# Non-local blocks in fp32: softmax denominators of two query pairs in one product, pooled products at every second pair

## The chip, the cores and the metric

The kernel runs on one core of a Trainium2 chip. The metric is the device time of one execution in microseconds (us), lower is better. Times come from repeated executions; one further execution was recorded by the hardware profiler. All data and all products are fp32.

The engines that matter here: PE multiplies matrices and writes PSUM, ACT (ScalarE) does exponentials, copies and biases, DVE (VectorE) does sums, maxima, reciprocals, and SP only issues DMAs. Each runs its own instructions strictly in the order in which the program lists them, and waits for the others by semaphores.

## The reference

Two layers are applied, one after the other, to x of shape (4, 128, 96, 96). A layer is (both layers alike, each with its own weights):

```python
g_x     = maxpool2(conv1x1(x, g_w, g_b)).reshape(b, CI, -1).transpose(0, 2, 1)    # 2304 keys x 64
theta_x = conv1x1(x, theta_w, theta_b).reshape(b, CI, -1).transpose(0, 2, 1)      # 9216 queries x 64
phi_x   = maxpool2(conv1x1(x, phi_w, phi_b)).reshape(b, CI, -1)                   # 64 x 2304 keys
f    = jnp.einsum('bqc,bck->bqk', theta_x, phi_x)
attn = jax.nn.softmax(f, axis=-1)
y    = jnp.einsum('bqk,bkc->bqc', attn, g_x)
W_y  = conv1x1(y, W_w, W_b)          # then a batch norm with fixed mean and variance
return W_y * inv + shift + x
```

So for each of 4 images and 2 layers: queries from all 9216 positions, keys and values from a 2 x 2 max-pooling of 9216 positions to 2304, attention over all keys, a projection, and the input added.

## The kernel before, in words

**Blocks, pairs, batches.** An image in a layer is a block; there are eight, in the order `ORDER`, so that an image's second layer never follows directly on its first. A block's 9216 queries are nine *pairs* (`NP`) of two times 512 queries, 72 pairs in all. A pair goes over the 2304 keys in 18 tiles of 128 (`NKT`), two at a time (`KB`): nine *batches* (`NB`), numbered j = 0 to 8.

**A batch.** `scores(k)` (L288 on PE) multiplies phi and theta into a PSUM tile `sc` of 128 x 1024, keys by queries, in four 64 x 64 tiles of the array side by side. ACT takes exp of it (L294), DVE adds the exp tile to a running `sum` (L298, L300). One batch later `values(k)` (L308) multiplies the exp tile by the pooled values into the accumulator `av`, again in four 64 x 64 tiles. There are two `sc` buffers, nine exp buffers, one `av`. PE's order in the main loop is: scores of batch t, then values of batch t-1, then what else is due.

**After a pair.** The softmax denominator is the sum over keys of `sum`: `denominators` (L321) multiplies it by a 128 x 64 matrix of ones, two products of 128 rows by 64 columns of the array side by side, one for each half of the queries; each result stands in 64 rows, so that it can multiply the output elementwise. ACT copies `av` to `halves` (L315), and copies the denominators to `rc` and adds them up for a later range check (L332). DVE adds the two halves (L345), takes the reciprocal of `rc` (L336, four pieces) and multiplies (L347); all that is in `normalise`. `note` (L341, ACT) adds up the reciprocals for the check. `project` (L356, PE) multiplies by W in 64 x 64 tiles, DVE adds shift and input (L362) in place into x, and in the second layer SP stores the piece (L367).

**The visit.** Everything that needs all 128 rows of the array at once comes together, once per pair, after the values of its batch 0 (`J_WINDOW`): up to three products of the next block's keys and values (`pooled`: L197 on PE into a `misc` PSUM tile, max-pooled by DVE at L203; there are two such tiles), the denominators of the pair before, and theta of the pair after (L275), which ACT copies out with its bias (L282). Denominators and theta share one `sc` buffer if there are such products in the visit, and take the two `misc` tiles otherwise. When enough of the next block is pooled, `spread` (three times per block, six transposes at L242, a DVE copy at L245, ACT at L232 and L235) brings it into its final layout, in the same place. The projection of the pair before follows in batch 4 (`J_PROJECT`).

```python
            if j == J_WINDOW:
                others = list(steps.pop(q % NP, []))
                for step in others[:2]:
                    step()
                visit(q, len(others) > 1)
                for step in others[2:]:
                    step()
                if q:
                    pairs[q - 1].normalise()
```

There are 24 products per block (`CC` = 384 columns each), three per visit (`CHUNKS`), so eight of a block's nine visits have some; the second block's come by fours in six visits. The last block's visits have none. The first block is prepared ahead of and within the first batches. SP's only work after the start is 39 stores and the loads of x, six pieces each (L94).

Of the kernel before, what the change touches and what calls it, by code (L numbers as in the profile page):

```python
# [9 lines left out]
F32 = mybir.dt.float32  # L10
I32 = mybir.dt.int32
AF = mybir.ActivationFunctionType
# [4 lines left out]
P = 128  # L17
# [16 lines left out]
NP = HW // PT  # L34
KB = 2
NB = NKT // KB
J_WINDOW, J_PROJECT = 0, 4
CHUNKS = 3
FIRST_CHUNKS, FIRST_GT = 4, 3
WARM = 5  # L40
ORDER = ((0, 0), (1, 0), (0, 1), (2, 0), (1, 1), (3, 0), (2, 1), (3, 1))
SHIFT = 35.0
SUM_MIN, SUM_MAX = 1e-20, 1e30
# [3 lines left out]
def shifted_blocks(ctx: ExitStack, tc: tile.TileContext, x: bass.AP, layers, out: bass.AP, flag):  # L47
# [38 lines left out]
    nc.vector.memset(ones, 1.0)  # L86
    dens = const.tile([P, len(ORDER) * NP], F32, name="dens")
    recs = const.tile([P, len(ORDER) * NP], F32, name="recs")

    def load_x(b, n=6):  # L90
        xt = xp.tile([C, HW], F32, tag="x", name=f"x_{b}")
        src = x[b].rearrange("c h w -> c (h w)")
        for i in range(n):
            nc.sync.dma_start(out=xt[:, ts(i, HW // n)], in_=src[:, ts(i, HW // n)])  # L94
        return xt
# [13 lines left out]
    class Layer:  # L109


        def __init__(self, l, p):
            self.l, self.p, self.col = l, p, {}
# [67 lines left out]
    class Block:  # L181
# [69 lines left out]
            self.spread_phi(i)  # L251
            self.spread_g(i)

        def key_steps(self, first, chunks):

            steps = {}
            for r in range(HW // CC):
                steps.setdefault(first + r // chunks, []).append(lambda r=r: self.pooled(r))
            for i in range(NKT // GT):
                last = ((i + 1) * GT * KT * 4 // CC - 1) // chunks  # L260
                steps.setdefault(first + last + 1, []).append(lambda i=i: self.spread(i))
            return steps

    class Pair:

# [12 lines left out]
                )  # L278

        def take_theta(self, ps):  # L280
            self.th = work.tile([P, QT], F32, tag="theta", name=f"theta_{self.name}")
            nc.scalar.activation(self.th, ps, AF.Identity, bias=self.blk.w.col["theta_b"])  # L282

        def scores(self, k):
            ps = ps_sc.tile([P, PT], F32, tag="sc", name=f"sc_{self.name}_{k}")
            for c in range(2):
                for h in range(2):
                    nc.tensor.matmul(  # L288
                        ps[ts(c, CI), ts(h, QT)],
                        lhsT=self.blk.phi[ts(h, CI), ts(2 * k + c, CI)],  # L290
                        rhs=self.th[ts(h, CI), :], start=True, stop=True,
                    )
            e = work.tile([P, PT], F32, tag="exp", name=f"exp_{self.name}_{k}", bufs=9)
            nc.scalar.activation(e, ps, AF.Exp, bias=nshift)  # L294
            self.es[k] = e
            if k == 1:
                self.sum = work.tile([P, PT], F32, tag="sum", name=f"sum_{self.name}")
                nc.vector.tensor_add(self.sum, self.es[0], e)  # L298
            elif k > 1 and not (self.last and k == NKT - 1):
                nc.vector.tensor_add(self.sum, self.sum, e)  # L300

        def values(self, k):
            if k == 0:
                self.av = ps_av.tile([P, PT], F32, tag="av", name=f"av_{self.name}")
            e = self.es[k]
            for h in range(2):
                for r in range(2):
                    nc.tensor.matmul(  # L308
                        self.av[ts(h, CI), ts(r, QT)], lhsT=self.blk.gT[ts(r, CI), k, :],
                        rhs=e[ts(r, CI), ts(h, QT)],  # L310
                        start=(k == 0), stop=(k == NKT - 1),
                    )
            if k == NKT - 1 and not self.last:
                self.halves = work.tile([P, PT], F32, tag="halves", name=f"halves_{self.name}", bufs=1)
                nc.scalar.copy(self.halves, self.av)  # L315

        def denominators(self, ps):
# [5 lines left out]
                        start=(i == 0), stop=(i == len(parts) - 1),  # L323
                    )

        def take_denominators(self, ps):
            self.den, n = ps, self.number
            self.rc = work.tile([P, QT], F32, tag="rc", name=f"rc_{self.name}", bufs=1)
            if self.last:
                self.inverses(ps)  # L330
            else:
                nc.scalar.activation(self.rc, ps, AF.Identity, accum_out=dens[:, n : n + 1])  # L332

        def inverses(self, src):
            for i in range(QT // P):
                nc.vector.reciprocal(self.rc[:, ts(i, P)], src[:, ts(i, P)])  # L336

        def note(self):
            n = self.number
            to = self.th if self.last else self.rc  # L340
            nc.scalar.activation(to, self.rc, AF.Identity, accum_out=recs[:, n : n + 1])  # L341

        def normalise(self):
            self.y = y = self.halves[:, :QT]
            nc.vector.tensor_add(y, y, self.halves[:, QT:])  # L345
            self.inverses(self.rc)
            nc.vector.tensor_mul(y, y, self.rc)  # L347

        def project(self):

# [15 lines left out]
                cols = ts(self.p, PT)  # L366
                nc.sync.dma_start(out=self.blk.store[:, cols], in_=self.blk.xt[:, cols])  # L367

        def finish(self, check, result):

            n = QT // 2
            halves = work.tile([P, PT], F32, tag="halves", name=f"halves_{self.name}", bufs=1)
            y, half = halves[:, :QT], halves[:, QT:]
            nc.scalar.copy(half, self.av[:, QT:])
            nc.vector.tensor_add(y, self.av[:, :QT], half)
            for i in range(2):
                nc.vector.tensor_mul(y[:, ts(i, n)], y[:, ts(i, n)], self.rc[:, ts(i, n)])
            nc.scalar.activation(
                self.th, self.den, AF.Identity, accum_out=dens[:, self.number : self.number + 1]
            )  # L380
            self.note()
            pss = [
                ps_sc.tile([P, PT], F32, tag="sc", name=f"W_ps_{self.name}_{i}") for i in range(2)
            ]
# [9 lines left out]
            for i in range(2):  # L394
# [8 lines left out]
                if i == 0:  # L403
                    result()

    ws = [Layer(l, p) for l, p in enumerate(layers)]
    ws[0].load_gphi((nc.scalar, nc.sync))
    xs = {0: load_x(0, 12)}
# [16 lines left out]
        store = out[b].rearrange("c h w -> c (h w)") if l else None  # L425
        blocks.append(Block(None, ws[l], store, f"{b}_{l}"))

    def begin(n, gt):

        b, l = ORDER[n]  # L430
        if b not in xs:
            xs[b] = load_x(b)
        blocks[n].xt = xs[b]
        blocks[n].begin_keys(gt)

    pairs = [Pair(blk, p, n * NP + p) for n, blk in enumerate(blocks) for p in range(NP)]
    total = len(pairs) * NB

    def visit(n, shared=True):

        if shared:
            ps = ps_sc.tile([P, PT], F32, tag="sc", name=f"den_theta_ps_{n}")
            den, th = ps[:, :QT], ps[:, QT:]
        else:
            den = ps_misc.tile([P, QT], F32, tag="misc", name=f"den_ps_{n}")
            th = ps_misc.tile([P, QT], F32, tag="misc", name=f"theta_ps_{n}")
        if n > 0:
            pairs[n - 1].denominators(den)
        if n + 1 < len(pairs):
            pairs[n + 1].theta(th)  # L450
        if n > 0:
            pairs[n - 1].take_denominators(den)
        if n + 1 < len(pairs):
            pairs[n + 1].take_theta(th)


    warm = ps_misc.tile([P, QT], F32, tag="misc", name="warm_ps")
    for i in range(WARM):
        nc.tensor.matmul(warm[:, :P], lhsT=ident, rhs=ident, start=True, stop=True)


    begin(0, FIRST_GT)
    b0 = blocks[0]
    ws[0].make_gphi()
    ws[0].make_theta()
    b0.pooled(0)
    b0.pooled(1)
    b0.pooled_2(2)
    first_cols()
    for w in ws:  # L470
        w.make_std()
    nc.scalar.preload_act_table(AF.Exp)
    b0.spread_phi(0)
    visit(-1)
    b0.pooled(4)
    b0.pooled(5)
    b0.pooled_2(6)
    b0.spread_phi(1)
    b0.spread_g(0)
    between = {0: 8, 1: 12, 3: 16, 4: 20}  # L480
    after = {
        0: [lambda: b0.spread_g(1)],
# [6 lines left out]
        NB: [ws[1].make_gphi, ws[1].make_theta],  # L489
        2 * NB: [ws[1].make_W, ws[1].make_shift],  # L490
    }
    steps = {}
    for t in range(total + 1):
        if t < total:
            q, j = divmod(t, NB)
            if q % NP == 0 and j == 0 and q // NP + 1 < len(blocks):
                begin(q // NP + 1, GT)
                plan = (2, FIRST_CHUNKS) if q == 0 else (0, CHUNKS)
                steps = blocks[q // NP + 1].key_steps(*plan)
            for k in range(j * KB, (j + 1) * KB):  # L500
                pairs[q].scores(k)
        if t in between:
            b0.pooled(between[t])
            b0.pooled(between[t] + 1)
            b0.pooled_2(between[t] + 2)
        if t:
            q, j = divmod(t - 1, NB)
            if j == J_PROJECT and q:
                pairs[q - 1].note()
                pairs[q - 1].project()  # L510
            if t <= total:
                for k in range(j * KB, (j + 1) * KB):
                    pairs[q].values(k)
            if t == total - 1:
                visit(len(pairs))
            if t == total:
                break
            if j == J_WINDOW:
                others = list(steps.pop(q % NP, []))
                for step in others[:2]:  # L520
                    step()
                visit(q, len(others) > 1)
                for step in others[2:]:
                    step()
                if q:
                    pairs[q - 1].normalise()
        for step in after.pop(t, []):
            step()

    good = const.tile([P, 2], F32, name="good")  # L530
    count = const.tile([1, 2], F32, name="count")
# [11 lines left out]
        nc.vector.tensor_scalar(count[:, 1:2], count[:, 0:1], 2.0 * P, None, ALU.is_lt)  # L543
        nc.vector.tensor_copy(flag, count[:, 1:2])

    pairs[-1].finish(check, result)


@with_exitstack
# [301 lines left out]
```

## Time and profile before

| | |
|---|---|
| time, median of 3 runs (lowest to highest) | 2609.92 us (2609.47 to 2610.31) |
| the profiled execution's own time | 2608.83 us |
| its span in the profile | 2606.8 us |
| DVE sum, one addition of 128 x 1024 (L300) | 1224 ns, x1151 |
| exp, one tile of 128 x 1024 (L294) | 1113 ns, x1296 |
| reciprocal, 128 x 128 (L336) | 908 ns, x284 |
| max-pooling of one product (L203) | 552 ns, x192 |
| granted clock of TensorE, mean | 0.999 of full speed |

How to read it: a timeline line gives the start and the duration in us, the engine, the line of the kernel, the operation and its operands, how many instructions are merged, and in brackets the idle time before and what ended it. `PE` rows are matmuls, `PEld` rows their weight loads, which run ahead. An fp32 matmul of the program is two matmuls in the profile. The ends of matmuls are modelled, so the distance from one start to the next is the more reliable measure of a matmul's time. Each profile line's "mean ns" is of one instruction; in 64 x 64 tiles four run at once, in 128 x 64 tiles two.

### The profile page before, as it was taken

The page shows a single profiled execution, that of the slowest core. Times are in us where ns is not written, and L with a number is a line of the kernel's source. Part 1 is how long each engine was busy: PE and PEld are TensorE (multiplying, and loading weights), DVE is VectorE, ACT ScalarE, POOL GpSimd, SP SyncE. Part 2 cuts the span into 40 slices and gives each one's busy share as a digit, 9 for nine tenths or more (in the row PEclk, how much of TensorE's full clock was granted, in tenths as well). Part 3 has the DMA queues.
Part 4 walks back from the last instruction along what each step waited for, and adds up shares of the span by engine and source line. Part 5 has one row for each costly group of instructions (what it writes and reads, how often), then busy time and mean ns, then how long its engine had stood idle before and what let it go on. Part 6 is the DMA issues. An engine that isn't in the chain of part 4 may idle for free.

```text
span 2606.8 us, 52190 instructions
## 1 busy us (share of the span) xinstructions
PE 2585.5 (99%) x22836; PEld 908.6 (35%) x22836; DVE 2036.2 (78%) x2069; ACT 1625.5 (62%) x1786; POOL 0.7 (0%) x6
## 2 busy tenths in 40 slices
PE   9999999999999999999999999999999999999998
PEld 3333333333333333333333333333333333333332
DVE  5777787777787777887778877778777788777777
ACT  4666666666666666666666666666666666666665
POOL 0000000000000000000000000000000000000000
PEclk9999999999999999999999999999999999999999
DMA  5000000000000002000000000000000000000000
GB/s 222 1 1 1 1 1 1 1 1 1 1 18 9 18 17 89 2 1 1 1 1 18 17 10 17 17 2 1 1 1 1 18 17 17 9 17 18 17 17 26
DMA packets 10974, 41.41 MB, mean 16 GB/s; under 512 B 1514, under 2 KB 2420, under 8 KB 10740
## 3 DMA queue, kind: packets, MB, share of 16 engines
q1 hardware_dynamic: 10572, 37.96, 3.7%
q8 instruction: 180, 2.95, 0.4%
q14 instruction: 54, 0.44, 0.1%
q10 hardware_dynamic: 168, 0.07, 0.0%
HBM read 19.14 MB, written 18.87 MB: 15 GB/s over the span
## 4 chain that ended last, share of the span: by engine, by line
PE 95%; DVE 2%; ACT 2%; issue 0%; DMA 0%; ACTq 0%; DVEq 0%
PE sc L288 42%; PE av L308 41%; PE gphi_ps L197 5%; PE W_ps L356 2%; PE den_theta_ps L321 2%; PE den_theta_ps L275 2%; ACT exp L294 1%; DVE sum L300 1%; PE theta_ps L275 1%; DVE sum L298 0%; PE den_ps L321 0%; ACT phi L232 0%; DVE centre L230 0%; ACT phi L235 0%; DVE gphi L203 0%
## 5 line engine op out<-in xcount | busy, mean ns | idle before, releaser
L294 ACT ACTIVATE exp<-sc,nshift 128x1024 f32<-128x1024 f32 x1296 | 1375.4, 1113 | 701.3 <-PE sc L288 700.7
L300 DVE TENSOR_TENSOR sum<-sum,exp 128x1024 f32<-128x1024 f32 x1151 | 1409.4, 1224 | 320.6 <-ACT exp L294 240.9
L288 PE MATMUL sc<-theta,phi 64*64 64x512 f32 x10368 | 1234.7, 591 | 5.5 <-ACT exp L294 4.6
L308 PE MATMUL av<-exp,gT 64*64 64x512 f32 x10368 | 1229.1, 589 | 0.0
L308 PEld LDWEIGHTS av<-exp,gT 64*64 64x64 f32 x10368 | 395.9, 133 | 716.5 <-issue 696.0
L288 PEld LDWEIGHTS sc<-theta,phi 64*64 64x64 f32 x10368 | 385.7, 133 | 721.5 <-issue 649.2
L336 DVE RECIPROCAL rc<-rc 128x128 f32<-128x128 f32 x284 | 240.2, 908 | 0.7
L298 DVE TENSOR_TENSOR sum<-exp,exp 128x1024 f32<-128x1024 f32 x72 | 88.2, 1226 | 136.8 <-ACT exp L294 136.8
L203 DVE TENSOR_REDUCE gphi<-gphi_ps 128x96 f32<-128x384 f32 x192 | 100.4, 552 | 95.0 <-PE gphi_ps L197 94.4
L332 ACT ACTIVATE rc<-den_theta_ps 128x512 f32<-128x512 f32 x54 | 32.3, 597 | 191.0 <-PE den_theta_ps L275 191.0
L197 PE MATMUL gphi_ps<-x,gphiT 128*64 128x384 f32 x768 | 148.5, 500 | 0.0
L362 DVE SCALAR_TENSOR_TENSOR x<-W_ps,shift,x 128x512 f32<-128x512 f32 x142 | 99.6, 743 | 0.0
L315 ACT COPY halves<-av 128x1024 f32<-128x1024 f32 x71 | 71.9, 1012 | 32.2 <-PE av L308 32.2
L197 PEld LDWEIGHTS gphi_ps<-x,gphiT 128*64 128x64 f32 x768 | 50.5, 138 | 107.9 <-issue 62.3
L356 PE MATMUL W_ps<-halves,WT 64*64 64x512 f32 x568 | 73.7, 589 | 0.0
L321 PE MATMUL den_theta_ps<-sum,ones 128*64 128x512 f32 x220 | 56.6, 593 | 0.0
L275 PE MATMUL den_theta_ps<-x,thetaT 128*64 128x512 f32 x216 | 55.5, 592 | 0.0
L347 DVE TENSOR_TENSOR halves<-halves,rc 128x512 f32<-128x512 f32 x71 | 49.1, 692 | 2.4
L345 DVE TENSOR_TENSOR halves<-halves 128x512 f32<-128x512 f32 x71 | 48.5, 683 | 0.1
L341 ACT ACTIVATE rc<-rc 128x512 f32<-128x512 f32 x71 | 44.5, 627 | 0.0
L356 PEld LDWEIGHTS W_ps<-halves,WT 64*64 64x64 f32 x568 | 21.7, 133 | 39.2 <-issue 38.9
L232 ACT ACTIVATE phi<-gphi,centre 64x768 f32<-64x768 f32 (+1 forms) x27 | 23.2, 860 | 9.0 <-DVE centre L231 8.5
(82 smaller groups left out, 263.4 us busy)
## 6 DMA issues: line engine op xcount, KB each, us to landing
out_dram<-x SPq DMA_DIRECT2D x35, 512.0 KB
x<-in_x_dram SPq DMA_DIRECT2D x18, 768.0 KB
x<-in_x_dram SPq DMA_DIRECT2D x12, 384.0 KB
out_dram<-x SPq DMA_DIRECT2D x4, 128.0 KB
gphi_nat<-in_L_conv_phi_w_dram SPq DMA_DIRECT2D x2, 32.0 KB
rows_other<-in_L_conv_g_b_dram SPq DMA_DIRECT2D x4, 0.2 KB
W_nat<-in_L_conv_W_w_dram SPq DMA_DIRECT2D x2, 32.0 KB
gphi_nat<-in_L_conv_g_w_dram ACTq DMA_DIRECT2D x1, 32.0 KB
```

The source lines that it names most:

```text
L197: nc.tensor.matmul(ps[ts(h, CI), :CC], lhsT=self.w.gphi[:, ts(h, CI)], rhs=self.xt[:, ts(r, CC)], start=True, stop=True,)
L203: nc.vector.tensor_reduce(self.gphi[:, ts(r, CC // 4)].rearrange("p (h w) -> p h w", w=W // 2), ps[:, :CC].rearrange("p (h a w b) -> p h w ...
L275: nc.tensor.matmul(ps[ts(h, CI), :], lhsT=self.blk.w.theta, rhs=self.blk.xt[:, ts(2 * self.p + h, QT)], start=True, stop=True,)
L288: nc.tensor.matmul(ps[ts(c, CI), ts(h, QT)], lhsT=self.blk.phi[ts(h, CI), ts(2 * k + c, CI)], rhs=self.th[ts(h, CI), :], start=True, stop= ...
L294: nc.scalar.activation(e, ps, AF.Exp, bias=nshift)
L298: nc.vector.tensor_add(self.sum, self.es[0], e)
L300: nc.vector.tensor_add(self.sum, self.sum, e)
L308: nc.tensor.matmul(self.av[ts(h, CI), ts(r, QT)], lhsT=self.blk.gT[ts(r, CI), k, :], rhs=e[ts(r, CI), ts(h, QT)], start=(k == 0), stop=(k ...
L321: nc.tensor.matmul(ps[ts(h, CI), :], lhsT=ones, rhs=part[:, ts(h, QT)], start=(i == 0), stop=(i == len(parts) - 1),)
L336: nc.vector.reciprocal(self.rc[:, ts(i, P)], src[:, ts(i, P)])
L356: nc.tensor.matmul(pss[h][ts(c, CI), :], lhsT=self.blk.w.W[ts(h, CI), ts(c, CI)], rhs=self.y[ts(h, CI), :], start=True, stop=True,)
L362: nc.vector.scalar_tensor_tensor(dst, pss[h], self.blk.w.shift, dst, op0=ALU.add, op1=ALU.add)
```

## The change

**Pairs of pairs.** A visit happens only at every second pair (q even), after the values of its batch 0. It serves two pairs at once: the denominators of pairs q-2 and q-1 and theta of pairs q+1 and q+2. It holds six products (`CHUNKS` = 6) where it held three, so each of the seven later blocks has four visits with products.

**Denominators.** The new class `Two` multiplies the two pairs' sums by 32 columns of ones: four products of 128 rows by 32 columns, one for each half of each pair, each result in 32 rows. One copy on ACT and one reciprocal of 128 x 512 on DVE (in the place of the first pair's `sum`) then serve both pairs. As a pair needs each half's reciprocals in 64 rows, eight DMAs on SP, each 32 rows of 2 KB within SBUF, copy them to the free half of each pair's `halves` tile.

**Order.** The reciprocals stand behind the pooling and the spreading on DVE. The range check's sum (`note`, ACT, in place over the reciprocals) and the first pair's multiplication come at batch 3, the second pair's at batch 5; the projections at batches 5 and 7. Spreads that would fall behind the last even pair of a block go to batch 5 of its last pair. The last pair but one has its denominators, reciprocals and projection by itself, as before. Buffers: exp 7 (9), `theta` 3 (2), `sum` 3 (2), `halves` 2 (1), and `rc` none of its own.

**Start.** The warm-up matmuls are 5 and 3 instead of 5, in the `av` tile; the first columns (biases and variances), the square roots and the loading of the exp table stand one step earlier; theta of the first pair has a tile of its own. The loads of x of images 2 and 3 are placed at pairs 4 and 31.

```diff
-J_WINDOW, J_PROJECT = 0, 4
-CHUNKS = 3
-FIRST_CHUNKS, FIRST_GT = 4, 3
-WARM = 5
+J_VISIT, J_NORMALISE, J_PROJECT = 0, (3, 5), (5, 7)
+CHUNKS = 6
+EXPS = 7
+FIRST_GT = 3
+WARM = (5, 3)
...
-            e = work.tile([P, PT], F32, tag="exp", name=f"exp_{self.name}_{k}", bufs=9)
+            e = work.tile([P, PT], F32, tag="exp", name=f"exp_{self.name}_{k}", bufs=EXPS)
...
+        def take_denominators(self, ps):
+
             n = self.number
-            to = self.th if self.last else self.rc
+            self.rc = self.sum[:, :QT]
+            nc.scalar.activation(self.rc, ps, AF.Identity, accum_out=dens[:, n : n + 1])
+
+        def note(self, to):
+            n = self.number
             nc.scalar.activation(to, self.rc, AF.Identity, accum_out=recs[:, n : n + 1])
 
+        def add_halves(self):
+            self.y = self.halves[:, :QT]
+            nc.vector.tensor_add(self.y, self.y, self.halves[:, QT:])
+
         def normalise(self):
-            self.y = y = self.halves[:, :QT]
-            nc.vector.tensor_add(y, y, self.halves[:, QT:])
-            self.inverses(self.rc)
-            nc.vector.tensor_mul(y, y, self.rc)
+            nc.vector.tensor_mul(self.y, self.y, self.rc)
...
+    class Two:
+
+
+        def __init__(self, one, two):
+            self.both = (one, two)
+
+        def denominators(self, ps):
+
+            for i, pair in enumerate(self.both):
+                for h in range(2):
+                    nc.tensor.matmul(
+                        ps[ts(2 * i + h, 32), :], lhsT=ones[:, :32],
+                        rhs=pair.sum[:, ts(h, QT)], start=True, stop=True,
+                    )
+
+        def take_denominators(self, ps):
+            self.both[0].take_denominators(ps)
+            self.rc = self.both[0].rc
+
+        def invert(self):
+
+            self.both[0].inverses(self.rc)
+            for i, pair in enumerate(self.both):
+                pair.add_halves()
+                pair.rc = pair.halves[:, QT:]
+                for h in range(2):
+                    for n in range(2):
+                        nc.sync.dma_start(
+                            out=pair.rc[ts(2 * h + n, 32), :], in_=self.rc[ts(2 * i + h, 32), :]
+                        )
+
+        def note(self):
+            n = self.both[0].number
+            nc.scalar.activation(self.rc, self.rc, AF.Identity, accum_out=recs[:, n : n + 1])
...
-    def visit(n, shared=True):
...
+    def visit(q, steps):
+
+
+
+        two = Two(pairs[q - 2], pairs[q - 1]) if q > 1 else None
+        later = pairs[q + 1 : q + 3]
+        steps = list(steps)
+        chunks = len(steps) > 1
+        if chunks:
+            for step in steps[:2]:
+                step()
+            ps = ps_sc.tile([P, PT], F32, tag="sc", name=f"den_theta_ps_{q}")
+            den, room = ps[:, :QT], ps[:, QT:]
         else:
-            den = ps_misc.tile([P, QT], F32, tag="misc", name=f"den_ps_{n}")
-            th = ps_misc.tile([P, QT], F32, tag="misc", name=f"theta_ps_{n}")
...
+            den = ps_misc.tile([P, QT], F32, tag="misc", name=f"den_ps_{q}")
+            room = ps_sc.tile([P, PT], F32, tag="sc", name=f"theta_ps_{q}_0")[:, :QT]
+        if two:
+            two.denominators(den)
+        later[0].theta(room)
+        if two:
+            two.take_denominators(den)
+        later[0].take_theta(room)
+        if chunks:
+            steps[2]()
+        if len(later) > 1:
+            room = ps_sc.tile([P, PT], F32, tag="sc", name=f"theta_ps_{q}_1")[:, :QT]
+            later[1].theta(room)
+            later[1].take_theta(room)
+        for step in steps[3 if chunks else 0 :]:
+            step()
+        if two:
+            two.invert()
+        return two
...
     for t in range(total + 1):
...
         if t:
             q, j = divmod(t - 1, NB)
-            if j == J_PROJECT and q:
-                pairs[q - 1].note()
-                pairs[q - 1].project()
+            if two and q % 2 == 0 and j in J_PROJECT:
+                two.both[J_PROJECT.index(j)].project()
...
                 for k in range(j * KB, (j + 1) * KB):
                     pairs[q].values(k)
...
+            if two and q % 2 == 0 and j in J_NORMALISE:
+                if j == J_NORMALISE[0]:
+                    two.note()
+                two.both[J_NORMALISE.index(j)].normalise()
...
+            if q % 2 == 0 and j == J_VISIT:
+                if q in begins:
+                    begin(begins[q])
+                two = visit(q, keys.pop(q, []))
```

## The prediction

> **What bounds the kernel now.** I read first the page's busy times and its chain of work that ended last, then the list of waits, then the timeline around one visit. In the page:
>
> ```profile
> PE 2585.5 (99%) x22836; PEld 908.6 (35%) x22836; DVE 2036.2 (78%) x2069; ACT 1625.5 (62%) x1786; POOL 0.7 (0%) x6
> PE 95%; DVE 2%; ACT 2%; issue 0%; DMA 0%; ACTq 0%; DVEq 0%
> ```
>
> PE is busy 99% of the span and holds 95% of the last chain. In the list of waits, PE's matmuls wait for exp 4.6 us in all. So only three things can shorten the run: less PE work, fewer bubbles between PE's instructions, a shorter start or end. DVE (78%) and ACT (62%) count only where PE ends up waiting for them. One visit with three products, in the chain of waits (start, us, what):
>
> ```profile
> 1006.00 1.44 PE gphi_ps L197 x8
> 1007.44 0.86 PE den_theta_ps L321 x4
> 1008.30 0.86 PE den_theta_ps L275 x4
> 1009.16 0.65 PE gphi_ps L197 x4
> 1009.80 1.88 PE sc L288 x16
> ```
>
> The denominators of one pair cost PE 0.86 us, theta 0.86 us, a product 0.64 us. The same visit in the timeline (PE, DVE and ACT lines):
>
> ```profile
> 1004.11 1.90 PE L308 MATMUL av<-exp,gT 64*64 64x512 f32 x16
> ...
> 1007.27 1.03 PE L321 MATMUL den_theta_ps<-sum,ones 128*64 128x512 f32 x4
> ...
> 1008.99 0.81 PE L197 MATMUL gphi_ps<-x,gphiT 128*64 128x384 f32 x4
> ...
> 1009.85 0.56 DVE L203 TENSOR_REDUCE gphi<-gphi_ps 128x96 f32<-128x384 f32 x1 [1.67 <-PE gphi_ps L197]
> 1010.33 0.68 DVE L345 TENSOR_TENSOR halves<-halves 128x512 f32<-128x512 f32 x1
> ...
> 1010.92 3.38 DVE L336 RECIPROCAL rc<-rc 128x128 f32<-128x128 f32 x4
> ...
> 1011.50 1.90 PE L308 MATMUL av<-exp,gT 64*64 64x512 f32 x16
> ...
> 1014.95 10.52 DVE L300 TENSOR_TENSOR sum<-sum,exp 128x1024 f32<-128x1024 f32 x8
> ```
>
> Scores or values of a batch take 1.72 us of PE from start to start (the timeline has scores at 1013.22 after values at 1011.50). The values that start at 1004.11 end at 1005.83; the two products before 1007.27 must start 1.29 earlier, at 1005.98: 0.15 us of nothing. On leaving, the last product ends at 1009.63 and scores start at 1011.50 - 1.72 = 1009.78: 0.15 again. I use 0.16 for each change between 64 x 64 and 128 x 64 tiles, because it closes the whole pair. The scores right after a visit, in neighbouring pairs of the chain of waits, first with three products and late in the run with none:
>
> ```profile
> 1941.93 1.88 PE sc L288 x16
> 1977.65 1.88 PE sc L288 x16
> ...
> 2399.69 1.88 PE sc L288 x16
> 2433.48 1.88 PE sc L288 x16
> ```
>
> Without products 33.79, against 9 x 3.43 + 0.86 (W) + 0.86 + 0.86 + 2 x 0.16 = 33.77; with three, 35.72, 1.93 more. PE's pairs are explained: there is no stall to remove (only a block's first spread holds exp up, seven times, and does so after the change too).
>
> **The change part by part.**
>
> **Denominators.** 71 single products (pairs 0 to 70) become 35 for two pairs and one for pair 70. If four 128 x 32 tiles run side by side as two 128 x 64 do, each visit costs 0.86: saved 35 x 0.86 = **30.1 us**. No 128 x 32 product is in the trace. The nearest row, 64 x 64 tiles, runs four at once (four loads per 0.43 us). Bounds: 30.1 saved, or nothing if they run two at a time.
>
> **Tile changes.** At first sight half the visits save half the changes: 72 x 0.32 = 23.0 becomes 36 visits and one for pair 70, 37 x 0.32 = 11.8, a gain of 11.2 us. Here a rule of the Trainium skill speaks against the change: "TensorEngine Tiling (Array Packing)", section Tiling Modes, says that changing the tiling mode, not just the tile, drains the array, and lists 128 x 32 and 128 x 64 as different modes. The trace shows the cost between two other modes (0.16) but not this one. By the rule 35 visits go in and out of 128 x 32 among theta and products: 28 visits with products have four changes, seven without have three (denominators come first), the visit of pair 0 and pair 70's have two: 28 x 0.64 + 7 x 0.48 + 2 x 0.32 = 21.9. Gain 1.1 instead of 11.2. I take the rule, priced by the row; the ends are 1.1 and 11.2. Four spreads leave their visits (those of blocks 1, 2, 4 and 6) and need one change more each: +0.6.
>
> **Six products on two tiles.** Products use two `misc` tiles in turn: the sixth needs the tile of the fourth, with no theta between. A product's max-pooling starts about 0.22 after its slot ends (slot end 1009.63, DVE 1009.85) and takes 0.56; PE starts some 0.1 later, so 0.88 where only the fifth product, 0.64, lies between: a stall of 0.24 in 28 visits, **+6.7 us** (0 if PE's slots hide it, 15 if DVE is a whole pooling late).
>
> **DVE.** 35 x 3.38 us of reciprocals go, all beside PE work: 0. After the visit DVE does one pooling, four reciprocals and two additions, until 0.78 + 3.4 + 1.4 = 5.6 us after the last product (call that end V), then sums at 10.52/8 = 1.315. The first multiplication comes after six of them, at V+13.5, done V+14.2. Its W product is due nine half batches after V, at 0.16 + 9 x 1.72 = V+15.6: 1.4 us of cover. The sum of exp tile 4 ends at V+6.9; with seven exp buffers exp 11 needs it at about V+12.5: covered.
>
> **ACT.** Fewer copies and notes; nothing on the path. But `note` moves to batch 3 and writes in place over the reciprocals, so it now waits for **all eight DMAs**, and every later exp is queued behind it on ACT, and PE behind the exps. SP has nothing else in its way: loads of x lie between visits, stores follow projections. SP starts when the first halves are added, V+4.9. A DMA's issue takes 3.03/6 = 0.5 us for the loads of x (L94), 0.33 for one store (L367), about 0.59 for a weight: the eighth is issued at V+4.9+7x0.5 = V+8.4. Copies within SBUF are not in the trace. The nearest row is 32 KB of theta weights, beside loads of x:
>
> ```profile
> 1.35 3.73 DMA theta_nat<-in_L_conv_theta_w_dram
> ```
>
> 3.73 us from issue to landing is the upper end. "DMA: Bandwidth & Descriptors", section Anatomy of one DMA, gives a fixed part of about 2.0 us (fitted on the GpSimd queue); that is the lower end. I take 2.5, nearer to the page, as no loads run beside: all landed at V+10.9 (ends: 4.9 + 7x0.33 + 2.0 = 9.2 and 4.9 + 7x0.6 + 3.7 = 12.8). When does PE notice? Scores 8 and 9 end at V+8.75, exp 9 at V+10.3, `note` lasts 0.83, exp 10 and 11 2.12, and PE needs the buffer of scores 11 at V+14.75. So landing by **V+11.7** costs nothing, and each us after it costs PE one in 28 visits. Seven visits without products have about 1.5 us more. Central: 0.
>
> **Start.** PE's first scores waited for theta: `[0.82 <-ACT theta L282]` at 15.39. With table load and columns a step earlier that bubble goes; next is PE's own transposes: -0.8. **End**: pair 70's projection ends two batches before the last sums, the final reciprocals follow as before: 0.
>
> **Sum.** -30.1 - 1.1 + 0.6 + 6.7 - 0.8 = -24.7. The profiled execution took 2608.83 (span 2606.8 and 2.0 around it), so 2584.1; the median of the runs is 1.1 above it: **2585.2 us**. A double period with products shrinks by only 0.62 us (0.86 - 0.24), one without by 1.0.
>
> **The rivals.**
>
> *The DMAs land late.* Place: `note` on ACT at batch 3. Price: 28 us per us of landing after V+11.7. It outweighs 24.7 from V+12.6. At the far end, V+12.8, 1.1 x 28 = 31 us are lost: 2616 us, slower. For it: eight issues in series on one queue and a margin of 0.8 us; against: the upper end is taken from a loaded queue. Chance of slower 0.10, of a partial loss (2590 to 2605) 0.12.
>
> *Going between 128 x 32 and 128 x 64 costs nothing*, both having 128 rows: 10.1 us better, 2575 us; with the pooling stall hidden too, 2568. For it: within a visit, products, denominators and theta follow each other without a bubble (but in one mode); against: the rule. Chance 0.20.
>
> *The change doesn't do what it says*: four 32-column products run two by two. Then -24.7 + 30.1 = +5.4: 2615 us. Against: 64 x 64 tiles run by four. Chance 0.04.
>
> *The expected case*, 2580 to 2590: 0.54.
>
> **How the numbers follow.** 0.2% is 5.2 us, about what can be told from no change here. Slower: late DMAs 0.10 and two-by-two 0.03 (of its 0.04): 0.13. Within 0.2%: the rim of both, 0.04. Faster 0.83. The range from 2570 to 2602 holds the expected case, most of the free tile changes and most of the partial losses; left out are some 0.2.
>
> **What would show it.** Right: a double period of about 70.8 us with products (71.4 before) and 66.6 without (67.6); denominators as 128*32, eight per visit in 0.86; bubbles of about 0.16 around them; PE waiting about 0.24 for a pooling at the sixth product; `note` waiting for a DMA at most some 0.6 us; no exp-caused stall in batch 4 to 6. Wrong: scores in batch 6 waiting for exp, with `note` held by a DMA (first rival); evenly spaced weight loads around the denominators (second); denominators of 1.7 us per visit (third).

## The result and the profile after

| | before | after |
|---|---|---|
| median of the runs (lowest to highest) | 2610.11 us (2609.47 to 2610.69, 4 runs) | 2583.66 us (2583.11 to 2585.79, 4 runs) |
| ratio to before, with its 95% interval | | 0.990 [0.9883, 0.9917] |
| the profiled execution's own time, and its span | 2608.83, 2606.8 us | 2585.79, 2583.7 us |
| PE, end of pair 0 to end of pair 70 | 2497.2 us | 2472.5 us |

The change saves 26.4 us by the medians. The profiled execution is the longest of the four of the changed kernel: the spans of the other three are 2581.1 to 2581.7 us. Some of that stands in its last microseconds: the span ends 6.2 us after the last addition on DVE (4.7 before). That is not part of what follows. The last row of the table is the part that can be compared piece by piece: it runs from the copy of `av` after pair 0 to that after pair 70 (L315 before, L311 after).

The busy line of the page after (engine, busy us, share of the span, instructions):

```profile
PE 2562.3 (99%) x22842; PEld 903.5 (35%) x22842; DVE 1919.3 (74%) x1931; ACT 1581.1 (61%) x1646; POOL 0.7 (0%) x6
```

PE is still what bounds the kernel. DVE lost 117 us and ACT 44 us of work, and the time did not follow them. Where PE's time went is read in the timeline. A visit with six products and no spread, that of pair 4 (start, us, engine, line, operation):

```profile
172.96 1.51 PE L200 MATMUL gphi_ps<-x,gphiT 128*64 128x384 f32 x8
...
174.40 1.06 PE L410 MATMUL den_theta_ps<-sum,ones 128*32 128x512 f32 x8
...
175.39 1.08 PE L271 MATMUL den_theta_ps<-x,thetaT 128*64 128x512 f32 x4
...
177.80 2.34 PE L200 MATMUL gphi_ps<-x,gphiT 128*64 128x384 f32 x12
...
179.28 0.20 PEld L200 LDWEIGHTS gphi_ps<-x,gphiT 128*64 128x64 f32 x4 [0.68 <-DVE gphi L206]
...
181.84 1.90 PE L304 MATMUL av<-exp,gT 64*64 64x512 f32 x16
...
184.65 4.95 SPq L427 DMA_DIRECT2D halves<-sum  x8
...
191.21 0.63 ACT L433 ACTIVATE sum<-sum 128x512 f32<-128x512 f32 x1 [0.94 <-DMA halves<-sum]
```

PE's order is: two products, denominators, first theta, a product, second theta (these two stand in the lines left out), three products. The eight matmuls of the denominators (four products, two matmuls each) start at 174.40 and theta's at 175.39. That is 0.99, of which 0.86 is put down to the product and 0.13 to the change of tile behind it; two by two, the products alone would have taken 1.72. The two products before end at 172.96 + 1.29 = 174.25, 0.15 ahead of the denominators. So four 32-column tiles do run side by side, and the way between 128 x 32 and 128 x 64 costs about what the way from 64 x 64 did (0.15). The weights of the sixth product wait for DVE's pooling (179.28). Scores start at 181.84 - 1.72 = 180.12; going back over one change and one product (0.16 and 0.64) the sixth product started at 179.32. The two before it were over at 177.80 + 1.29 = 179.09, so the stall is 0.23.

A double period runs from the end of one odd pair to the end of the next, by ACT's copies of `av`; the one around the visit of pair 10 runs from the copy of pair 9 to that of pair 11. Before:

```profile
393.12 1.01 ACT L315 COPY halves<-av 128x1024 f32<-128x1024 f32 x1 [0.45 <-PE av L308]
...
464.57 1.01 ACT L315 COPY halves<-av 128x1024 f32<-128x1024 f32 x1 [0.46 <-PE av L308]
```

and after:

```profile
385.12 1.01 ACT L311 COPY halves<-av 128x1024 f32<-128x1024 f32 x1 [0.46 <-PE av L304]
...
455.93 1.01 ACT L311 COPY halves<-av 128x1024 f32<-128x1024 f32 x1 [0.46 <-PE av L304]
```

Double periods over the whole run, in us (a visit with products and no spread is called plain below; before, it is two pairs with three products each):

| visit with | before | after | forecast after |
|---|---|---|---|
| products, no spread (13, from pair 4 on) | 71.44 | 70.80, but for pairs 28 and 30 | about 70.8 |
| no products, no spread | 67.57 | 66.54 | 66.6 |
| products and the first spread of a block | 73.00 | 72.35 | |
| products and the second spread | 71.96 | 71.31 | |
| a third spread adds | 0.99 | 0.53 in a visit (pairs 26, 44, 62); at a block's last pair 0.68 (pairs 17, 35, 53) and 1.00 (pair 8) | as before, 0.16 more at a block's last pair |

Eight double periods after are longer than their kind: pairs 14, 22, 28, 30, 58 by 0.3 to 0.9 us, 24, 26, 62 by 0.1 to 0.5, together 3.9. In each the eight copies of the reciprocals landed late. Pair 28:

```profile
1040.50 5.88 SPq L427 DMA_DIRECT2D halves<-sum  x8
...
1048.00 0.63 ACT L433 ACTIVATE sum<-sum 128x512 f32<-128x512 f32 x1 [1.89 <-DVE sum L296]
...
1049.78 0.21 PEld L284 LDWEIGHTS sc<-theta,phi 64*64 64x64 f32 x8 [0.79 <-ACT exp L290]
1049.78 2.09 PE L284 MATMUL sc<-theta,phi 64*64 64x512 f32 x16
...
1050.79 0.21 PEld L284 LDWEIGHTS sc<-theta,phi 64*64 64x64 f32 x8 [0.80 <-ACT exp L290]
```

Eight issues took 5.88 us instead of 4.95. The note (L433) starts 7.5 us after the first issue; in pair 4 it was 6.56. The profile names a DVE sum as its releaser, but the note needs nothing of that sum, and it does need the eight copies. (Where an instruction waits for several semaphores, the profile names the one that happened to come last by its own times.) What shows the cost is the weight load of the next scores, at 1049.78 and again at 1050.79, waiting for exp. The scores' two groups take 2.09 where they otherwise take 1.90.

Pair 30 is late in another way. Its eight issues take the usual time, and the note starts 8.1 us after the first; here six loads of x (L97) are issued right behind the eighth copy:

```profile
1111.58 4.99 SPq L427 DMA_DIRECT2D halves<-sum  x8
1116.62 3.86 SPq L97 DMA_DIRECT2D x<-in_x_dram  x6
```

### The profile page after: what moved, and what is told of

Its sections match the earlier page's. It is cut to its first block, busy times and chain, and to the rows that moved or that the text cites. A ratio compares the mean times of both kernels' runs of the same rounds, so it can differ in the third digit from the quotient of the medians.

```text
span 2583.7 us, 52594 instructions
## 1 busy us (share of the span) xinstructions
PE 2562.3 (99%) x22842; PEld 903.5 (35%) x22842; DVE 1919.3 (74%) x1931; ACT 1581.1 (61%) x1646; POOL 0.7 (0%) x6
## 4 chain that ended last, share of the span: by engine, by line
## 5 line engine op out<-in xcount | busy, mean ns | idle before, releaser
L284 PEld LDWEIGHTS sc<-theta,phi 64*64 64x64 f32 x10368 | 392.1, 133 | 714.5 <-issue 659.4
L324 DVE RECIPROCAL sum<-sum 128x128 f32<-128x128 f32 x144 | 121.7, 907 | 2.8 <-ACT sum L330 2.7
L311 ACT COPY halves<-av 128x1024 f32<-128x1024 f32 x71 | 71.9, 1012 | 32.4 <-PE av L304 32.4
L330 ACT ACTIVATE sum<-den_theta_ps 128x512 f32<-128x512 f32 x28 | 16.7, 597 | 107.1 <-PE den_theta_ps L271 107.1
L433 ACT ACTIVATE sum<-sum 128x512 f32<-128x512 f32 x35 | 22.1, 631 | 45.5 <-DMA halves<-sum 33.5
L341 DVE TENSOR_TENSOR halves<-halves 128x512 f32<-128x512 f32 x70 | 47.8, 682 | 0.0
L271 PE MATMUL theta_ps<-x,thetaT 128*64 128x512 f32 x176 | 44.4, 597 | 0.0
L338 DVE TENSOR_TENSOR halves<-halves 128x512 f32<-128x512 f32 x71 | 43.4, 652 | 0.0
L271 PE MATMUL den_theta_ps<-x,thetaT 128*64 128x512 f32 x112 | 30.2, 618 | 0.0
```

The source lines that it names most:

```text
L271: nc.tensor.matmul(ps[ts(h, CI), :], lhsT=self.blk.w.theta, rhs=self.blk.xt[:, ts(2 * self.p + h, QT)], start=True, stop=True,)
L284: nc.tensor.matmul(ps[ts(c, CI), ts(h, QT)], lhsT=self.blk.phi[ts(h, CI), ts(2 * k + c, CI)], rhs=self.th[ts(h, CI), :], start=True, stop= ...
```

## The experiments

All are edits of the changed kernel except one of the kernel before. "Medians" are of the runs beside the kernel before on the same chip. The first is the measure for the next three.

**The changed kernel again.** 

> The changed kernel itself, as the measure for the runs beside it: 2583.7 us, and a profile with the denominators in 128*32 tiles, 70.8 us for two pairs with products, and some eight or nine visits in which the last of the eight copies lands more than 7.0 us after the first was issued and PE then waits 0.3 to 0.8 us for exp.

2584.38 us (2583.87 to 2585.49), ratio 0.990 [0.9888, 0.9921]. Pairs 14, 22, 24, 28, 30 and 58 are late again, and 60 with them; 26 and 62 are not. So the lateness keeps to certain stretches of the run, but not wholly to the same visits.

**The note later.**

```diff
-                if j == J_NORMALISE[0]:
+                if j == J_NORMALISE[1]:
                     two.note()
```

> Only the note over the reciprocals moves, from batch 3 to batch 5. Theory (in visits whose copies land late, note holds the exps behind it and PE loses 3 to 4 us in all): 2580 us, note waits for no DMA, visits with products and no spread all at 70.8 us. Rival (what those visits lose comes from DVE or elsewhere, and the note is hidden anyway): 2583.7 us as before.

2580.45 us (2579.79 to 2581.46): 3.9 us less. All plain double periods now take 70.79 to 70.81 us, those of pairs 28 and 30 too, and from pair 6 on all with a first spread 72.35 or 72.36. In the list of waits (engine, line, waited for: us in total, times, longest) the changed kernel has

```profile
PEld sc L284 <- ACT exp L290: 44.6, 68, 1.5
...
ACT sum L433 <- DMA halves<-sum: 33.5, 27, 2.4
```

and with the later note the first is

```profile
PEld sc L284 <- ACT exp L290: 19.9, 20, 1.5
```

and the second is not there. So the late copies reach PE only through the note on ACT. The multiplications on DVE also need the copies, and had time enough where they were.

**Denominators ahead of the products.**

```diff
         if chunks:
-            for step in steps[:2]:
-                step()
             ps = ps_sc.tile([P, PT], F32, tag="sc", name=f"den_theta_ps_{q}")
...
             two.denominators(den)
+        if chunks:
+            for step in steps[:2]:
+                step()
         later[0].theta(room)
```

> The denominators go ahead of the first two products, so that the array goes 64x64, 128x32, 128x64, 64x64: three changes of tile instead of four in 28 visits. Theory (each change costs 0.16 us): 28 x 0.16 = 4.5 us less, 2579 us. Rival (the gap beside the denominators is a wait for ACT's or DVE's semaphore and moves with them): no change, 2583.7 us.

2579.66 us (2579.46 to 2580.6): 4.7 us less. The timeline of its visit at pair 4:

```profile
172.26 1.07 PE L410 MATMUL den_theta_ps<-sum,ones 128*32 128x512 f32 x8
173.26 1.51 PE L200 MATMUL gphi_ps<-x,gphiT 128*64 128x384 f32 x8
174.60 1.03 PE L271 MATMUL den_theta_ps<-x,thetaT 128*64 128x512 f32 x4
```

From products to theta it is now 1.34, of which 1.29 is the two products: no change of tile there. Plain double periods fall from 70.80 to 70.65, and those with products and spreads by as much. So the gap goes with the change of tile, and not with a semaphore that the denominators wait for.

**The second theta later.**

```diff
             steps[2]()
+            steps[3]()
...
-        for step in steps[3 if chunks else 0 :]:
+        for step in steps[4 if chunks else 0 :]:
```

> The second theta goes from behind the third product to behind the fourth, so that 1.5 us of PE work lie between the fourth product and the sixth, which takes its tile. Theory (sixth product waits 0.23 us for the pooling of the fourth, 28 times): 6.5 us less, 2577 us, no wait for DVE in the visit. Rival (the wait only moves to another product, or the later theta holds the scores up): 2582 to 2585 us.

2577.58 us (2577.47 to 2579.2): 6.8 us less, plain double periods 70.56. The wait for the pooling was, first in the changed kernel, then here:

```profile
PEld gphi_ps L200 <- DVE gphi L206: 19.4, 29, 0.7
```

```profile
PEld gphi_ps L200 <- DVE gphi L206: 8.3, 29, 0.3
```

What is left, 0.3 us at a time, is the weight load alone waiting; in the visit of pair 4 the matmuls follow on each other.

**The three together** (the three diffs above in one kernel).

> The three small moves together: note at batch 5, denominators first, second theta behind the fourth product. Theory (three separate terms of PE time): 3.5 + 4.5 + 6.5 = 14.5 us less than the changed kernel, 2569 us. Rival (they overlap, since a visit that ends earlier for PE only meets the same pooling, reciprocals or copies sooner): 2573 us or more.

2570.67 us (2570.18 to 2571.2), ratio to before 0.985 [0.9837, 0.9867]. That is 38.7 us below the kernel before on the same chip (2609.41); the changed kernel was 26.4 and 24.6 below in its two measurements. So the three bring 12 to 14 us together, where their single gains add up to 15.4. Plain double periods are 70.41, 0.39 below the changed kernel's, which is the 0.15 and the 0.23. It is the fastest version here.

**Denominators in 64 columns.** Visits stay merged, the 32-column product and the copies go:

```diff
-J_VISIT, J_NORMALISE, J_PROJECT = 0, (3, 5), (5, 7)
+J_VISIT, J_NORMALISE, J_PROJECT = 0, (3, 4), (5, 8)
...
         if two:
-            two.denominators(den)
+            two.both[0].denominators(den)
         later[0].theta(room)
         if two:
-            two.take_denominators(den)
+            two.both[0].take_denominators(den)
...
+        den, room = ps[:, :QT], ps[:, QT:]
+        if two:
+            two.both[1].denominators(den)
...
-            self.both[0].inverses(self.rc)
+            self.both[0].inverses(self.both[0].rc)
+            for pair in self.both:
+                pair.add_halves()
...
+                one = two.both[J_NORMALISE.index(j)]
+                one.note(one.rc)
+                one.normalise()
+                if j == J_NORMALISE[0]:
+                    two.both[1].inverses(two.both[1].rc)
```

> Visits stay at every second pair, but each pair has its own denominators in 128x64 tiles and its own reciprocals, without the copies within SBUF; the second pair's reciprocals come at batch 3, its multiplication at batch 4, the projections at batches 5 and 8. Theory (32 columns save one product of 0.86 us per visit and cost two tile changes of 0.16, one where there are no products; late copies cost 3.5 us): 28 x 0.54 + 7 x 0.70 - 3.5 = 16.5 us more than the changed kernel, 2600 us. Rival (the gain came from merging the visits, not from the columns): 2584 us or less. If the second reciprocals make DVE late for the projections: above 2605 us.

2632.21 us, ratio 1.009 [1.0077, 1.0104]. The experiment failed, since it put a new wait in. The second note, at batch 4, stood on ACT waiting for the reciprocals that DVE began at batch 3:

```profile
197.92 0.63 ACT L334 ACTIVATE sum<-sum 128x512 f32<-128x512 f32 x1 [3.25 <-DVE sum L324]
...
199.70 2.09 PE L284 MATMUL sc<-theta,phi 64*64 64x512 f32 x16 [0.35 <-ACT exp L290]
```

It is the same trap as the late copies: an instruction whose result nobody needs soon, on the engine that PE waits for. So it was run again with the notes at batches 6 and 7:

```diff
-                one.note(one.rc)
                 one.normalise()
...
+            if two and q % 2 == 0 and j in (6, 7):
+                one = two.both[j - 6]
+                one.note(one.rc)
```

> den64 once more, with the two notes at batches 6 and 7 instead of 3 and 4, since there the second note waited on ACT for the second pair's reciprocals and held the exps behind it. Theory (32 columns save 0.86 us of PE per visit and cost tile changes): 2600 us, 16.5 more than the changed kernel. Rival (the gain came from merging the visits, not from the columns): 2584 us or less. Rival (DVE, with twice the reciprocals, is late for projections or pooling): above 2605 us.

2610.1 us (2607.81 to 2612.33), ratio to before 1.0005 [0.9996, 1.0013]: about 26 us above the changed kernel, not 16.5. Plain double periods are 71.37, 0.57 more than 70.80 (0.54 expected: 0.86 less two changes of tile), so the theory of the product holds where nothing else moves. The total falls into the range set for the rival that DVE is late, but most of the excess is not DVE's. In visits without products theta's ACT copy now comes behind the second denominators' and holds the scores (double periods 67.84, 1.30 more where 0.70 was expected). Once the projection, now at batch 8, waited 3.1 us for the tile of a third spread, and that double period is 4.4 longer. With the 3.9 us of late copies gone, 28 x 0.57 + 7 x 1.30 + 4.4 - 3.9 = 25.6 us. One such wait of the scores, and that of the projection:

```profile
2399.80 1.09 PE L284 MATMUL sc<-theta,phi 64*64 64x512 f32 x8 [0.35 <-ACT theta L278]
```

```profile
346.32 0.65 PE L350 MATMUL W_ps<-halves,WT 64*64 64x512 f32 x3 [3.13 <-DVE gT L248]
```

Merging visits without merging the denominators brought nothing in this form; another form was not tried.

**More copies.** Twelve or sixteen instead of eight, the same bytes:

```diff
-                    for n in range(2):
+                    for n in range(4):
                         nc.sync.dma_start(
-                            out=pair.rc[ts(2 * h + n, 32), :], in_=self.rc[ts(2 * i + h, 32), :]
+                            out=pair.rc[ts(4 * h + n, 16), :],
+                            in_=self.rc[ts(2 * (2 * i + h) + n % 2, 16), :],
                         )
```

(for sixteen; for twelve only the second pair's copies are cut in this way).

> The copies are cut in two: sixteen of 16 rows instead of eight of 32. Theory (copies are issued one after the other at 0.62 us each and all landed at V+11.3 now, and what lands after V+11.7 is paid by PE one to one through note and the exps behind it): landing at about V+16.2, 4.5 us in each of 28 visits and some 3 in the other seven, 2730 us. Rival (exp buffers take up the delay): 2584 to 2600 us.

> Twelve copies: the first pair's in four of 32 rows as before, the second pair's in eight of 16. Theory (each copy more is 0.68 us on the queue; all landed near V+14.0; PE pays what lies beyond V+11.7 one to one, and stays short enough of the idle time after which the clock fell with sixteen copies): about 2.3 us in 28 visits and some 0.7 in the other seven, 2650 to 2656 us. Rival (part of the delay is taken up by the buffers): below 2625 us. If the clock falls here too: above 2680 us.

Sixteen: 2812.26 us (two runs), ratio 1.078 [1.0759, 1.0798]. Twelve: 2676.66 us (2673.23 to 2677.45), ratio 1.025 [1.024, 1.0268]. Both are slower than either kernel, so the rival that buffers take the delay up falls. But both are more than the theory had, by some 80 and 20 us. With twelve copies two visits show why. In the first (pair 12) the note starts 9.44 us after the first issue, in the second (pair 38) 9.63 us:

```profile
493.94 2.09 PE L284 MATMUL sc<-theta,phi 64*64 64x512 f32 x16 [1.83 <-ACT exp L290]
495.85 1.04 PE L350 MATMUL W_ps<-halves,WT 64*64 64x512 f32 x8
...
1460.62 3.42 PE L284 MATMUL sc<-theta,phi 64*64 64x512 f32 x16 [2.02 <-ACT exp L290]
1463.80 1.33 PE L350 MATMUL W_ps<-halves,WT 64*64 64x512 f32 x8
```

After 1.83 us of idleness the scores take 2.09, as after short waits; after 2.02 they take 3.42, and the projection takes longer too. The stages around the two (window, us, busy time and count of PE, PEld, DVE, ACT, POOL, granted clock, DMA share, GB/s) show TensorE's clock:

```profile
493.90:496.00 2.10, 2.06 (x20) 0.72 (x24) 1.98 (x2) 1.89 (x2) 0.00 (x0) 1.00 0.00 0
...
1460.60:1464.10 3.50, 3.48 (x20) 1.21 (x24) 3.03 (x3) 2.10 (x3) 0.00 (x0) 0.55 0.00 0
```

1.00 in the first, 0.55 in the second. Plain visits with twelve copies whose scores keep the full clock lose 1.8 to 2.2 us (72.63 to 73.00 against 70.80), where landing at V+13.8 to V+14.1 was to cost 2.1 to 2.4: one to one, as forecast. In the other plain visits (pairs 28, 30, 36, 38) the scores are slow after waits of 2.02 to 2.77 us, and these lose 3.9 to 4.8. So the clock fell here too, if not often enough for the 2680 us that had been set for that case.

**Five exp buffers.**

```diff
-EXPS = 7
+EXPS = 5
```

> Five exp buffers instead of seven. Theory (the sum of exp tile 4 ends at V+6.9, the exp that would need its buffer starts at V+9.2 with five): no change, 2583.7 us, within 1. Rival (buffers were what set EXPS, fewer hold exp up behind the reciprocals): over 2590 us.

2584.38 us (2582.97 to 2585.42): no change, as expected.

**The kernel before, third spread behind its visit.**

```diff
-                for step in others[:2]:
+                first = 2 if len(others) > 1 else 0
+                for step in others[:first]:
                     step()
                 visit(q, len(others) > 1)
-                for step in others[2:]:
+                for step in others[first:]:
```

> The kernel before, with the third spread of each block put behind the visit instead of ahead of it, as the changed kernel has it. Theory (in the kernel before, theta of that visit waited for the tile that the spread's DVE copy held, about 0.46 us, seven times): 3.2 us less, 2606.9 us. Rival (the third spread costs the same wherever it stands): 2610.1 us.

2606.05 us (2605.15 to 2608.39), ratio to before 0.9988 [0.9981, 0.9994], 3.4 us less. The seven double periods with a third spread are each shorter by 0.47 (about 70.50 to 70.03 for pairs 8, 16, 26 and 44 among them), no other changes by more than 0.01. In the kernel before the list of waits had a line, not shown ahead of the prediction, that said so:

```profile
PEld theta_ps L275 <- DVE gT L245: 7.9, 7, 1.1
```

In the kernel with the spread behind the visit that line is gone.

## Why the prediction was right, point by point

The direction, the size (24.7 us forecast, 26.4 by the medians, 23.1 between the profiled spans) and the likeliest case were right, and so was the mechanism of the main terms. Two steps were wrong by 3 and 4 us, in opposite directions: that the sum came out so near is in part luck.

| step | forecast, us | measured, us | from |
|---|---|---|---|
| denominators | -30.1 | 0.86 per visit for four products: -30.1 | timeline after |
| tile changes | -1.1 | about -1.1: 0.13 to 0.15 each beside 128 x 32, as elsewhere; 0.15 per visit when one is taken away | timeline, denominators first |
| six products on two tiles | +6.7 | 0.23 per visit, +6.5; 6.8 by the median | second theta later |
| spreads | +0.6 | -2.4 | double periods |
| note behind the copies | 0 | +3.9 | note later |
| start | -0.8 | -1.4: pair 0's copy of `av` starts at 65.68 instead of 66.21, with one theta (0.86) more ahead of it | ACT's copies |
| end | 0 | +2.0 in the profiled execution, 1.5 of it behind DVE's last addition | span |

The measured steps add up to -22.6, against 23.1 between the profiled spans. Between the ends of pairs 0 and 70 the kernel gained 24.6 us; 0.86 of these are only pair 2's theta, which now stands in the visit of pair 0.

*Denominators, tile changes, six products* hold to a few tenths of a us, in double periods to a few hundredths. The rival that four 32-column products run two by two falls: they take 0.86. The rival that going between 128 x 32 and 128 x 64 is free falls too, by the timeline and by the experiment that takes one such change away.

*Spreads.* The step that failed is the sentence "PE's pairs are explained: there is no stall to remove". It was checked on pairs with products and no spread, and on pairs with neither. A third spread in the kernel before stood ahead of denominators and theta in its visit, held one of the two `misc` tiles until DVE had copied it, and theta waited: seven spreads cost 0.99 us each, of which moving it behind gives back 0.47. The change moves it behind too, and puts the visit's theta in other tiles. It now costs 0.53 where it stands in a visit and 0.68 at three blocks' last pairs (0.15 more, the forecast's extra change of tile). At pair 8, where the first projection comes right behind it, it costs 1.00; what makes the difference there was not tested. Before, the seven blocks' three spreads cost 7 x (1.56 + 0.52 + 0.99) = 21.5 over double periods without spreads; after, 7 x (1.55 + 0.52) + 3 x 0.53 + 3 x 0.68 + 1.00 = 19.1.

*The note.* The mechanism and the place were right, and the size of two terms was off. An issue was taken as 0.5 us and is 4.95/8 = 0.62, and 0.74 in pair 28; from the eighth issue to all landed was taken as 2.5 and is about 2.2 (191.21 less 184.65 and 7 x 0.62). So the usual landing is V+11.3 instead of V+10.9 (the first issue is at V+4.7), still inside the limit, and the late ones are at about V+12 and beyond.

PE starts to lose about 7.2 us after the first issue, V+11.9 (forecast V+11.7), and from there one to one: pair 20, 7.04, loses nothing; 24, 7.33, 0.1; 28, 7.50, 0.3; 30, 8.08, 0.85. In visits with a first spread the limit is 6.9: pair 6, 6.90, loses nothing; 58, 7.41, 0.5; 22, 7.76, 0.8. Both limits are the same with five exp buffers. The sign that the note would wait at most some 0.6 us for a DMA was set too low: in pair 4 it waits 0.94 and PE loses nothing.

What makes the copies of some visits late is not settled. In seven of the eight the issues alone take 5.7 to 6.3 us instead of 5.0. In pair 30 they do not, and there the prediction's "loads of x lie between visits" is wrong: SP issues them right behind the copies, and the copies land 3.1 us after the last issue has ended instead of 1.6. The same loads stand behind the copies in pair 2, which loses nothing (6.85), and in pair 30 of the kernel with the denominators first the note started after 6.75; so these loads can be no more than part of the cause.

*The price of the first rival* was set at 28 us per us and holds, in what was run, while PE's wait stays short of about 2 us. With twelve copies the plain visits whose scores were slowed lost 1.5 to 1.6 us more than their lateness.

*DVE's and ACT's freed time, exp buffers, the reciprocals' place* were put at nothing, and no loss was found there. Five buffers do as well as seven.

## What to carry to other kernels

When the bounding engine's time per period can be added up from its own instructions to a hundredth, do it for every kind of period, those with a rare step too; the stall that was missed was in the list of waits, seven times, 7.9 us in all. Small instructions that nobody needs soon, as a range check, still wait in order: put them where what they wait for has long landed, since behind them stands what the bounding engine needs. Of a chain of small copies like this one count the issues, not the bytes alone, and look at the late ones, not the usual one.

## What the runs showed of the hardware beyond that

Small copies within SBUF cost by number: eight of 64 KB took 4.95 us to issue (0.62 each), sixteen of 32 KB 9.99 (0.62 each) in undisturbed visits. The note that waits for them started about 1.6 us after the last issue had ended, in most visits.

The clock of TensorE fell after short waits in a run that is otherwise 99% busy. With twelve copies, all 27 waits for exp up to 1.96 us were followed by scores of 2.09 us; of the 14 from 2.02 to 3.06 us, 11 were followed by slower ones (2.71 to 3.60 us). With sixteen, all 33 from 3.35 us on were (2.76 to 3.69), and of two between 2 and 3 us one was (2.54, not 2.79). The Trainium skill, "TensorE: Matmul & The Clock Gate", section Why this matters for your kernels, has idle gaps of more than about 3 us for this; here 2.02 us was already enough in some cases, and the measurement decides. What sets the exceptions apart was not tested.
